# A 512-step recurrent cell: five bf16-part steps of eight instead of four, and other shares of the input's products

## The chip, the core and the metric

The kernel runs on one core of a Trainium2 chip. The metric is the time of one execution on the device, in microseconds (us); the kernel before takes 1638.1 us, the median of 3 runs (1637.6 to 1639.26). Its profile is one such execution, of 1637.59 us.

The engines that matter are TensorE (PE: matmuls, and PEld, its weight loads), VectorE (DVE), ScalarE (ACT), GpSimd (POOL) and SyncE (SP, which issues most DMAs).

## The reference

Eight sequences of 512 steps go through a gated cell with 512 hidden units; the result is added to the input.

```python
def step(h, x_t):
    fused = sigmoid(concatenate([x_t, h], -1) @ w_W + w_b)
    hidden_state, output_state = split(fused, 2, axis=-1)     # r and z below
    memory_state = x_t @ wx_W + wx_b + hidden_state * (h @ wh_W + wh_b)
    h_new = output_state * h + (1.0 - output_state) * tanh(memory_state)
    return h_new, h_new
_, hs = scan(step, h0, swapaxes(x, 0, 1))
out = x + swapaxes(hs, 0, 1)
```

What needs x alone can be computed ahead. What needs h (three products of 512 x 512 in each step: for r, for z and for the memory) cannot start before the step before has ended.

## The kernel before

**Steps, groups, octets.** The main loop runs over the 512 steps i. Four steps make a group and share banks of the accumulator memory (PSUM): their eight batch rows each lie below one another in 32 rows. Two groups make an octet. Below, o is the octet's number (0 to 63) and u the step's place in it (0 to 7); the group of u = 0 to 3 is called even, that of u = 4 to 7 odd.

**The products with h.** The 512 units are in four chunks k (the contraction) and four column groups j (the output, 32 rows of PSUM each, one beside the other on the PE array). For each k and j the weights have 384 columns, in three banks: A (192: z, r and memory of half A of the units), B (128: r and memory of half B) and C (64: z of half B). `ORDER` fixes the order in each step: A0 B0 A1 A2 A3 B1 B2 B3 C0 C1 C2 C3, where the digit is k. A0 and B0 need the new state's first chunk, A1 its second, and so on. The trace counts two MATMULs and two weight loads for each fp32 product.

**C in parts.** `in_parts(i)` tells in which steps C is made otherwise: the state and the weights are each split into three bf16 parts. The state's parts (`split`) are the left operand: 3 parts of 8 batch rows, 24 columns, loaded once per k and j. The weights' three parts (`high(wb)`, `w2`, `w3`) are each run against it: the first by `mm`, the other two by `kept` (line 219 of the kernel before), which does not load the left operand again. The result lies in 24 rows, and a TENSOR_REDUCE on DVE adds the three (`tzs<-tzB`). For that a step needs 64 columns of its own in bank `cs`, `cell(i)`; steps in fp32 of the odd group share 64 columns. Before, steps u = 0 to 3 are made in parts from step 24 on. `split` is made on POOL at the end of the step before, four TENSOR_TENSORs (two for each half of the units); `w2` and `w3` are made once on POOL, a pair in each of the steps 12 to 19.

**x in shares.** The products with x of a whole octet are made ahead, by a scheme with seven products where eight would be needed (`product`, `SLOTS`): seven slots of two products, of 384 columns each, 2688 columns in all. `SHARE` gives the columns that each step of the octet computes, behind C; `x_step` walks along them. A share that crosses the end of a slot becomes two pieces. The sums between the products lie on ACT and DVE (copies and additions of 64 x 384), and `spread`, `spread_c` and `turn_x` bring the finished rows to where the steps start: `spread_c` writes the rows of one step, chosen by a mask, into its cell for C.

**One step after the last product A.** DVE transposes A's three pieces (`tr<-A`, `md1A<-A`, `tz<-A`), ACT takes the sigmoids, DVE combines (`m`, two scans), ACT takes tanh, DVE makes the new state of half A (`hT<-hd0A`, chunks 0 and 1), and the same follows for half B out of banks B and C (`hT<-hd0B`, chunks 2 and 3). PE works on B, C and the x share meanwhile.

**What sets the order.** Nothing is reordered: `Flow` records the operations as the program is written, works out the semaphore waits from the memory that they touch, and issues them in that order on each engine. So almost every instruction carries line 255 (257 in the changed kernel), that of the issuing loop, and must be told apart by its tiles. An access to a PSUM bank also waits for the last access of another engine to the same rows of that bank.

Of the kernel before, what the change touches and what calls it, by code (L numbers as in the profile page):

```python
# [15 lines left out]
NQ = 4  # L16
GS = 4
HS = 12
B = 8
HU = 64  # L20
# [24 lines left out]
    [("P7", 0), ("P6", 1)],  # L45
]

SHARE = [384, 384, 384, 384, 288, 288, 288, 288]

XP = {"A": slice(0, 192), "X": slice(192, 320), "C": slice(320, 384), "B": slice(384, 512)}  # L50

# [213 lines left out]
def tile_cond_rnn_residual(  # L265
# [42 lines left out]
    T = NCH * TC  # L308
    NG = T // GS
    LAST = NG // 2 - 1  # L310
# [70 lines left out]
    NH = 2 * GS  # L381
# [40 lines left out]
    def state(hf, i, slot=2):  # L422
# [4 lines left out]
    cs = psum.tile([P, 512], F32, name="cs")  # L427
    wide = [{n: psum.tile([P, 512], F32, name=f"{n}{q}") for n in "AB"} for q in range(2)]
    banks = [
        {"A": wide[q]["A"][:, : BANKS["A"]],  # L430
         "B": wide[q]["B"][:, : BANKS["B"]],
         "C": cs[:, GS * HU : GS * HU + HU]}
        for q in range(2)
    ]
    xps = [psum.tile([P, 512], F32, name=f"xp{q}") for q in range(2)]
# [3 lines left out]
    def high(t_):  # L439
        return t_.bitcast(BF16)  # L440
# [41 lines left out]
    def keep(g):  # L482

        nc.vector.tensor_tensor(
            source(g)[:, XC], (piece if g == 2 else xps[g % 2])[:, XC], bias[:, XC], ALU.add
        )

    def source(g):

        return xps[g % 2] if g // 2 == LAST else (even, odd)[g % 2]  # L490

    def spread(g, names):

        for n in names:
            nc.scalar.copy(banks[g % 2][n], source(g)[:, XP[n]])

    def cell(i):
        return cs[:, HU * (i % GS) : HU * (i % GS) + HU] if i // GS % 2 == 0 else banks[1]["C"]

    def in_parts(i):  # L500
        return 3 * NH <= i < T and i // GS % 2 == 0

    def spread_c(g, steps_):

        for s in steps_:
            nc.scalar.activation(
                cell(GS * g + s), source(g)[:, XP["C"]], AF.Copy, scale=mask[:, s, :1]
            )

    def turn_x(g, hf):  # L510

        c0 = XP["X"].start + HU * hf
        nc.vector.transpose(
            md1[hf][g % 2][:, :, :, 1].rearrange("p n c -> p c n"), source(g)[:, c0 : c0 + HU]
        )

    def reg(r, c=XC):
        return xps[r[0]][r[1], c]
# [18 lines left out]
    def x_sum(o, n):  # L537

        t_ = [q[o % 2] for q in sx]
        a, b, op = [  # L540
            (x_half(o, 1, 0), x_half(o, 1, 1), ALU.add),
            (t_[0], x_half(o, 0, 0), ALU.subtract),
            (x_half(o, 0, 0), x_half(o, 1, 0), ALU.subtract),
            (x_half(o, 0, 1), t_[1], ALU.subtract),
        ][n]
        nc.gpsimd.tensor_tensor(t_[n], a, b, op)

    def product(o, name, k, c0, c1):

        if not 2 <= o < LAST:  # L550
            return
        t_ = [q[o % 2] for q in sx]
        to, lhs, rhs = {
            "P1": (AL, lambda: x_half(o, 0, 0), wx_of(0, 0)),
            "P2": (DE, lambda: t_[0], tw[0]),
            "P3": (BE, lambda: t_[1], tw[1]),
            "P4": (AL, lambda: x_half(o, 0, 1), wx_of(1, 0)),
            "P5": (GA, lambda: t_[2], tw[2]),
            "P6": (BE, lambda: t_[3], wx_of(1, 1)),
            "P7": (GA, lambda: x_half(o, 1, 1), tw[3]),  # L560
            "E": (None, lambda: t_[2], tw[2]),
        }[name]
        for j in range(2):
            r = slice(32 * j, 32 * j + 32)
            out_ = eps[r, c0:c1] if to is None else reg(to, slice(XC.start + c0, XC.start + c1))[r]
            mm(out_, lhs()[:, k], rhs[:, k, j, c0:c1], start=to is None and c0 == 0)
# [17 lines left out]

    def x_step(o, u):

        at = sum((SHARE * 2)[5 : u if u > 4 else u + 8]) - SHARE[5] // 3
        o += 2 if u > 4 else 1
        end = at + SHARE[u]
        while at < end:  # L590
            n, c0 = divmod(at, W)
            c1 = min(W, c0 + end - at)
            for pair_, (name, k) in enumerate(SLOTS[n % 7]):
                product(o + n // 7 - (n % 7 == 0 and pair_ == 0), name, k, c0, c1)
            at += c1 - c0
# [27 lines left out]
    for i in range(T):  # L623
# [8 lines left out]
        for n in (ORDER if i else FIRST).split():  # L632
            if n == "x":
                take(first[3], 1)
                continue
            bank, k = n[0], int(n[1])
            lhsT = hs[i % NH][:, k, :32, 2]
            for j in range(NQ):
                if bank == "C" and in_parts(i):
                    parts(cell(i)[32 * j : 32 * j + 24], i, k, j)  # L640
                else:
                    to = cell(i) if bank == "C" else ps[bank]
                    mm(to[32 * j : 32 * j + 32, :], lhsT, wh(bank, k, j))
        if T - 17 <= i < T - 5:
            take(last[i >= T - 11], 1)
        elif i > 4:
            x_step(*divmod(i, 2 * GS))
# [42 lines left out]
        def turn_z(hf):  # L690
            if hf and in_parts(i):
                tz = work.tile([P, 2, B], F32, tag="tzs", name=f"tzs_{i}")
                nc.vector.tensor_reduce(
                    tz, tzb[0].rearrange("p c (u b) -> p c b u", u=4), mybir.AxisListType.X, ALU.add
                )
            else:
                tz, _ = turned("z", hf)
            if hf == 0:
                inst = nc.vector.memset(idle[:, IDLE - 1 :], 0.0).ins
                nc.after(inst, h_done[0])  # L700
            act(hd0[hf][i % 2][:, :, :, 2].rearrange("p n c -> p c n"),
                tz,
                AF.Sigmoid,
                scale=-1.0,
            )
# [24 lines left out]
        o, u = divmod(i, 2 * GS)  # L730
# [24 lines left out]
        update(1, 1)  # L755
        if 0 < o < LAST and u == 1:
            spread(2 * o + 1, "C")
        if nxt and u in (6, 7):
            spread_c(2 * o + 2, (2 * u - 12, 2 * u - 11))
        for hf in range(2 if i < T - 1 else 0):  # L760
            act(state(hf, i + 1, 0), state(hf, i + 1), AF.Copy)
            if in_parts(i + 1):
# [6 lines left out]
                    ALU.subtract,  # L769
                )  # L770
                nc.gpsimd.tensor_tensor(t_[:, :, 2], t_[:, :, 0], high(t_)[:, :, 0, 1::2], ALU.subtract)
        if NH + GS <= i < NH + GS + 2 * NQ:
            k, n = (i - NH - GS) // 2, slice(i % 2 * 2, i % 2 * 2 + 2)
            for to, t_ in ((w2, wb[:, :, :, :HU]), (w3, w2)):
                nc.gpsimd.tensor_tensor(
                    to[:, k, n], t_[:, k, n], high(t_)[:, k, n, 1::2], ALU.subtract
                )
# [8 lines left out]
        if o == LAST:  # L786
            if u == 2:
                spread(2 * o + 1, "AB")
                turn_x(2 * o + 1, 0)
                turn_x(2 * o + 1, 1)  # L790
            elif u == 3:
                spread(2 * o + 1, "C")
        elif u == 0:
            if o == 0:
                spread(1, "A")
            if sums:
                nc.scalar.copy(reg(BE), reg(AL))
                nc.scalar.copy(both[LO], reg(DE))
                x_sum(o + 1, 3)
            turn_x(2 * o + 1, 0)  # L800
            turn_x(2 * o + 1, 1)
        elif u == 1:
            if sums:
                nc.scalar.copy(more[HI], eps)
            spread(2 * o + 1, "BC" if o == 0 else "A")
        elif u == 2:
            if sums:
                nc.vector.tensor_tensor(reg(GA), reg(BE), more[HI], ALU.add)
                nc.scalar.copy(even[LO, XC], reg(AL))
            if o:  # L810
                spread(2 * o + 1, "B")
        elif u == 3:
            if sums:
                nc.vector.tensor_tensor(odd[HI, XC], reg(GA), both[LO], ALU.add)
                nc.scalar.copy(both[HI], reg(DE))
            if two:
                x_sum(o + 2, 2)
        elif u == 4:
            if o == 0:
                keep(3)  # L820
            if two:
                nc.scalar.copy(reg(AL), bias[LO, XC])
                x_sum(o + 2, 0)
        elif u == 5:
            if sums:
                nc.vector.tensor_tensor(even[HI, XC], reg(BE), both[HI], ALU.add)
            if two:
                nc.scalar.copy(reg(DE), step_bias[HI])
        elif u == 6 and nxt:
            spread(2 * o + 2, "AB")  # L830
            turn_x(2 * o + 2, 0)
        elif u == 7 and nxt:
            if o:
                nc.scalar.copy(odd[LO, XC], reg(GA))
            turn_x(2 * o + 2, 1)
            if two:
                x_sum(o + 2, 1)
# [107 lines left out]
```

## Time and profile before

| what | value |
|---|---|
| median of 3 runs | 1638.1 us |
| the profiled execution | 1637.59 us |
| its span, first to last instruction | 1635.5 us |
| TensorE busy | 1625.4 us (99%) |
| its weight loads | 1397.4 us (85%) |
| ACT / DVE / POOL busy | 1254.0 / 1235.8 / 531.8 us |
| granted TensorE clock | 1.000 |
| DMA, mean over the span | 19 GB/s |

Some 2.1 us of the profiled execution lie outside the span. A busy PE is not a PE at its peak: ends of matmuls are modelled. The step's length is best read from the starts of `tr<-A`, the first thing that DVE does when bank A is finished: there is one in each step, and the time from one to the next holds the rest of the step's own work (B, C, x) and the next step's A. "Length of step u" below means that.

### The profile page before, as it was taken

What the parts mean: (1) busy time and instruction counts of PE and PEld (TensorE: products, weight loads), DVE (VectorE), ACT (ScalarE), POOL (GpSimd) and SP (SyncE); (2) the same over time, 40 slices, a digit from 0 to 9 for tenths busy, and PEclk for the clock granted to TensorE, in tenths of its full rate; (3) what the DMA queues carried; (4) which work ended last, traced back from release to release, by engine and by line L of the source; (5) the groups of instructions that cost most, each with busy time, mean ns of one, the idle gap of its engine ahead of it and who ended that gap; (6) DMA issues with size and microseconds to landing.
All of it is one profiled execution on the core that took longest, in us unless ns stands there. A gap on an engine that the chain in (4) does not pass through costs nothing.

```text
span 1635.5 us, 127307 instructions
## 1 busy us (share of the span) xinstructions
PE 1625.4 (99%) x58202; PEld 1397.4 (85%) x50394; DVE 1235.8 (76%) x9433; ACT 1254.0 (77%) x6188; POOL 531.8 (33%) x2272
## 2 busy tenths in 40 slices
PE   8999999999999999999999999999999999999998
PEld 5988898988888888888888888888888888988887
DVE  7777777777777777777777777777777777777776
ACT  4777777778777777777777777777777777777775
POOL 1323323333233333332333333323333333333332
PEclk9999999999999999999999999999999999999999
DMA  4000000000000000000000000000000000000000
GB/s 185 12 14 18 15 15 14 18 15 14 15 18 15 15 14 18 15 15 15 17 15 15 15 18 14 15 15 18 14 15 15 17 15 15 15 18 10 10 10 11
DMA packets 37297, 31.25 MB, mean 19 GB/s; under 512 B 4084, under 2 KB 35060, under 8 KB 36600
## 3 DMA queue, kind: packets, MB, share of 16 engines
q1 hardware_dynamic: 36576, 22.89, 4.5%
q8 instruction: 425, 6.96, 1.7%
q14 instruction: 144, 1.18, 0.2%
q10 hardware_dynamic: 152, 0.22, 0.0%
HBM read 14.70 MB, written 8.39 MB: 14 GB/s over the span
## 4 chain that ended last, share of the span: by engine, by line
PE 98%; DVE 1%; DMA 0%; ACT 0%; issue 0%; DVEq 0%; ACTq 0%; SPq 0%
PE A L255 41%; PE B L255 27%; PE xp L255 17%; PE cs L255 9%; PE cs L219 4%; PE eps L255 1%; DMA head<-in_xh_dram 0%; DVE tr L255 0%; DVE m L255 0%; DVE tw L255 0%; DVE hT L255 0%; DVE md1A L255 0%; DVE tz L255 0%; DVE md1B L255 0%; DVE even L255 0%
## 5 line engine op out<-in xcount | busy, mean ns | idle before, releaser
L255 PE MATMUL A<-wa,hT 128*32 128x192 f32 x16384 | 872.3, 327 | 3.2 <-DVE hT L255 3.1
L255 PEld LDWEIGHTS A<-wa,hT 128*32 128x32 f32 x16384 | 549.4, 122 | 189.8 <-DVE hT L255 132.1
L255 PE MATMUL B<-wb,hT 128*32 128x128 f32 x16384 | 652.0, 273 | 0.0
L255 PEld LDWEIGHTS B<-wb,hT 128*32 128x32 f32 x16384 | 542.5, 122 | 19.9 <-DMA wb<-in_wb_dram 0.3
L255 POOL TENSOR_TENSOR ot<-xin,hT 128x16 f32<-128x16 f32 x991 | 224.1, 250 | 598.8 <-DVE hT L255 596.8
L255 ACT ACTIVATE hT<-m 128x8 f32<-128x8 f32 x2048 | 349.2, 208 | 65.0 <-DVE m L255 64.1
L255 DVE STREAM_TRANSPOSE tr<-A 128x64 f32<-128x64 f32 x512 | 127.9, 250 | 291.9 <-PE A L255 285.8
L255 PE MATMUL xp<-tw,sx 128*32 128x384 f32 (+2 forms) x1464 | 264.0, 433 | 0.0
L255 POOL TENSOR_TENSOR split<-hT 128x32 f32<-128x32 f32 x488 | 126.0, 258 | 410.0 <-DVE m L255 397.9
L255 ACT ACTIVATE hT<-hT 128x16 f32<-128x16 f32 x1022 | 210.3, 225 | 50.1 <-DVE hT L255 47.8
L255 ACT ACTIVATE md0A<-tr 128x16 f32<-128x16 f32 x512 | 112.2, 219 | 165.4 <-DVE tr L255 158.8
L255 DVE TENSOR_TENSOR_SCAN hT<-hd0B,hT 128x24 f32<-128x24 f32 x1024 | 179.5, 204 | 75.7 <-ACT hT L255 52.4
L255 PE MATMUL xp<-wx,xin 128*32 128x384 f32 (+4 forms) x1348 | 218.3, 413 | 0.0
L255 DVE TENSOR_TENSOR_SCAN hT<-hd0A,hT 128x24 f32<-128x24 f32 x1024 | 198.3, 194 | 0.0
L255 PE MATMUL cs<-wb,hT 128*32 128x64 f32 x8576 | 173.0, 219 | 0.0
L255 PEld LDWEIGHTS cs<-wb,hT 128*32 128x32 f32 x8576 | 161.4, 122 | 0.0
L255 DVE TENSOR_TENSOR_SCAN m<-md0A,md1A 128x16 f32<-128x16 f32 x1024 | 142.3, 181 | 6.9
L255 DVE TENSOR_TENSOR_SCAN m<-md0B,md1B 128x16 f32<-128x16 f32 x1024 | 145.0, 163 | 0.6 <-issue 0.4
L255 ACT ACTIVATE hd0A<-tz 128x16 f32<-128x16 f32 x512 | 116.0, 227 | 20.9
L219 PE MATMUL cs<-w,split 128*24 128x64 bf16 x7808 | 129.9, 192 | 0.0
L255 PE MATMUL cs<-wb,split 128*24 128x64 bf16 x3904 | 122.2, 192 | 0.0
L255 POOL TENSOR_TENSOR split<-split 128x16 f32<-128x16 f32 x488 | 105.2, 216 | 38.2
(101 smaller groups left out, 2216.0 us busy)
## 6 DMA issues: line engine op xcount, KB each, us to landing
out_dram<-ot SPq DMA_DIRECT2D x128, 64.0 KB, 1.6
xin<-in_x_dram SPq DMA_DIRECT2D x112, 64.0 KB, 2.4
wx<-in_wx_dram SPq DMA_DIRECT2D x4, 768.0 KB, 7.5
wa<-in_wa_dram SPq DMA_DIRECT2D x4, 384.0 KB, 10.1
wb<-in_wb_dram SPq DMA_DIRECT2D x1, 1152.0 KB, 13.4
xin<-in_x_dram SPq DMA_DIRECT2D x3, 256.0 KB, 3.1
wb<-in_wb_dram SPq DMA_DIRECT2D x1, 384.0 KB, 13.8
head<-in_xh_dram ACTq DMA_DIRECT2D x1, 208.0 KB, 5.6
```

What stands on the lines that cost most here:

```text
L219: return t.add_instruction(mybir.InstMatmult(name=self.nc.get_next_instruction_name(), ins=[t.lower_ap(rhs), t.lower_ap(lhsT)], outs=[t.lo ...
L255: inst = getattr(self, item.op, getattr(engine, item.op, None))(*item.args, **item.kw)
```

## The change

Three edits. First, C of the odd group's first step (u = 4) is also made in parts. It has a cell of its own for that in `cs`, the fp32 steps' shared columns move 64 to the right, and `spread_c` writes that step's x rows into its cell (a further ACTIVATE in each octet, behind the updates of u = 2; in octet 0 in u = 1 and in the last one in u = 3). Second, the shares of x: 384 columns in u = 4 as in u = 0 to 3, and 256 in u = 5, 6 and 7; the start of the walk moves by 96 columns, so that u = 0 to 4 now fill one slot each. Third, the weights' parts are made in steps 8 to 15, and parts are used from step 16 on.

```diff
-SHARE = [384, 384, 384, 384, 288, 288, 288, 288]
+SHARE = [384, 384, 384, 384, 384, 256, 256, 256]
+
+EARLY = 0
...
-         "C": cs[:, GS * HU : GS * HU + HU]}
+         "C": cs[:, (GS + 1) * HU : (GS + 2) * HU]}
...
     def cell(i):
-        return cs[:, HU * (i % GS) : HU * (i % GS) + HU] if i // GS % 2 == 0 else banks[1]["C"]
+        n = i % NH
+        return cs[:, HU * n : HU * n + HU] if n <= GS else banks[1]["C"]
 
     def in_parts(i):
-        return 3 * NH <= i < T and i // GS % 2 == 0
+        return 2 * NH <= i < T and i % NH <= GS
...
-        at = sum((SHARE * 2)[5 : u if u > 4 else u + 8]) - SHARE[5] // 3
+        at = sum((SHARE * 2)[5 : u if u > 4 else u + 8]) - EARLY
...
         if 0 < o < LAST and u == 1:
             spread(2 * o + 1, "C")
+        if 0 < o < LAST and u == 2:
+            spread_c(2 * o + 1, (0,))
...
-        if NH + GS <= i < NH + GS + 2 * NQ:
-            k, n = (i - NH - GS) // 2, slice(i % 2 * 2, i % 2 * 2 + 2)
+        if NH <= i < NH + 2 * NQ:
+            k, n = (i - NH) // 2, slice(i % 2 * 2, i % 2 * 2 + 2)
...
             elif u == 3:
                 spread(2 * o + 1, "C")
+                spread_c(2 * o + 1, (0,))
...
             spread(2 * o + 1, "BC" if o == 0 else "A")
+            if o == 0:
+                spread_c(1, (0,))
```

Two places show what moves. The first is PE's queue from u = 4 on in an octet in the middle. Before, with `hT_71` the state of u = 4 and `hT_72` that of u = 5, `cs` bank C, `xp` and `eps` the banks of the x products:

```order
L255 MATMUL cs<-wb,hT_71 32x64 x16
L255 MATMUL xp_121<-tw_101,xin_138 32x288 x2
L255 MATMUL xp_120<-wx,sx_109 32x288 x2
L255 MATMUL A_118<-wa,hT_72 32x192 x4
L255 MATMUL B_119<-wb,hT_72 32x128 x4
L255 MATMUL A_118<-wa,hT_72 32x192 x12
L255 MATMUL B_119<-wb,hT_72 32x128 x12
L255 MATMUL cs<-wb,hT_72 32x64 x16
L255 MATMUL xp_121<-tw_101,xin_138 32x96 x2
L255 MATMUL xp_120<-wx,sx_109 32x96 x2
L255 MATMUL xp_121<-tw_101,xin_138 32x192 x2
L255 MATMUL eps<-tw_100,sx_106 32x192 x2
```

In the changed kernel the same stretch, from the last three of the 48 matmuls of u = 4's C (`split_75` the state's parts, `w_77` and `w_78` the weights' second and third part):

```order
L257 MATMUL cs<-wb,split_75 24x64
L221 MATMUL cs<-w_77,split_75 24x64
L221 MATMUL cs<-w_78,split_75 24x64
L257 MATMUL xp_121<-tw_101,xin_138 32x384 x2
L257 MATMUL xp_120<-wx,sx_109 32x384 x2
L257 MATMUL A_118<-wa,hT_72 32x192 x4
L257 MATMUL B_119<-wb,hT_72 32x128 x4
L257 MATMUL A_118<-wa,hT_72 32x192 x12
L257 MATMUL B_119<-wb,hT_72 32x128 x12
L257 MATMUL cs<-wb,hT_72 32x64 x16
L257 MATMUL xp_121<-tw_101,xin_138 32x256 x2
L257 MATMUL eps<-tw_100,sx_106 32x256 x2
```

The 16 fp32 products of u = 4's C became 48 in bf16, its x share went from 288 to 384 columns, and that of u = 5 from 288 in two pieces to 256 in one.

The second place is ACT's queue at the end of u = 2, from the last tanh (`hT_69<-m`) on; `md0A<-tr` is the first sigmoid of u = 3. Before:

```order
L255 ACTIVATE hT_69<-m_2_140 128x8
L255 ACTIVATE hT_70<-hT_70 128x8x2 x2
L255 COPY even<-xp_120 64x384
L255 COPY B_119<-odd 128x128
L255 ACTIVATE md0A_80<-tr_3_148 128x2x8
```

In the changed kernel:

```order
L257 ACTIVATE hT_69<-m_2_140 128x8
L257 ACTIVATE cs<-odd,mask 128x64
L257 ACTIVATE hT_70<-hT_70 128x8x2 x2
L257 COPY even<-xp_120 64x384
L257 COPY B_119<-odd 128x128
L257 ACTIVATE md0A_80<-tr_3_148 128x2x8
```

One ACTIVATE, the x rows of u = 4's cell, stands ahead of the two copies of the state.

## The prediction

> **What bounds the kernel now.** I read the page first: is one engine full, and does the chain that ended last stay on it?
>
> ```profile
> span 1635.5 us, 127307 instructions
> PE 1625.4 (99%) x58202; PEld 1397.4 (85%) x50394; DVE 1235.8 (76%) x9433; ACT 1254.0 (77%) x6188; POOL 531.8 (33%) x2272
> PE 98%; DVE 1%; DMA 0%; ACT 0%; issue 0%; DVEq 0%; ACTq 0%; SPq 0%
> ```
>
> The chain lies on PE for 98%. That says that PE sets the length of most steps, but not that each would shrink with PE's work: below PE's queue runs a loop through DVE and ACT (A, transposes, sigmoids, state, next A), and a step can't be shorter than that. So I next looked for the length of each step u, by the starts of `tr<-A` in DVE's timeline. This is octet 20 (first start: u = 0):
>
> ```profile
> 525.60 0.25 DVE L255 STREAM_TRANSPOSE tr<-A 128x64 f32<-128x64 f32 x1 [0.80 <-PE A L255]
> 528.79 0.25 DVE L255 STREAM_TRANSPOSE tr<-A 128x64 f32<-128x64 f32 x1 [0.55 <-PE A L255]
> 531.97 0.25 DVE L255 STREAM_TRANSPOSE tr<-A 128x64 f32<-128x64 f32 x1 [0.81 <-PE A L255]
> 535.14 0.25 DVE L255 STREAM_TRANSPOSE tr<-A 128x64 f32<-128x64 f32 x1 [0.17 <-PE A L255]
> 538.33 0.25 DVE L255 STREAM_TRANSPOSE tr<-A 128x64 f32<-128x64 f32 x1
> 541.43 0.25 DVE L255 STREAM_TRANSPOSE tr<-A 128x64 f32<-128x64 f32 x1 [0.96 <-PE A L255]
> 544.54 0.25 DVE L255 STREAM_TRANSPOSE tr<-A 128x64 f32<-128x64 f32 x1 [0.28 <-PE A L255]
> 547.65 0.25 DVE L255 STREAM_TRANSPOSE tr<-A 128x64 f32<-128x64 f32 x1 [0.82 <-PE A L255]
> 550.76 0.25 DVE L255 STREAM_TRANSPOSE tr<-A 128x64 f32<-128x64 f32 x1 [0.81 <-PE A L255]
> ```
>
> The four steps in parts with 384 columns take 538.33 - 525.60 = 12.73, 3.18 each; the four in fp32 with 288 take 3.10, 3.11, 3.11, 3.11, 12.43 in all. What PE does in them shows the chain of waits, for u = 4 (fp32) and then for u = 1 (parts; its rows between are C's single matmuls):
>
> ```profile
> 538.92 0.45 PE cs L255 x29
> 539.37 0.49 PE xp L255 x8
> 539.85 0.33 PE A L255 x8
> ```
>
> ```profile
> 529.38 0.01 PE cs L255 x2
> ...
> 529.74 0.65 PE xp L255 x8
> ```
>
> C costs 0.45 in fp32 and 529.74 - 529.38 = 0.36 in parts; 288 columns of x cost 0.49, 384 cost 0.65.
>
> A price for a column comes from steps that differ in nothing else. In octets 1 and 2 all steps are fp32; here are a step of 384 columns (the first pair of starts) and one of 288 (the second):
>
> ```profile
> 71.03 0.25 DVE L255 STREAM_TRANSPOSE tr<-A 128x64 f32<-128x64 f32 x1 [0.83 <-PE A L255]
> 74.30 0.25 DVE L255 STREAM_TRANSPOSE tr<-A 128x64 f32<-128x64 f32 x1 [0.86 <-PE A L255]
> ```
>
> ```profile
> 58.60 0.25 DVE L255 STREAM_TRANSPOSE tr<-A 128x64 f32<-128x64 f32 x1 [0.42 <-PE A L255]
> 61.71 0.25 DVE L255 STREAM_TRANSPOSE tr<-A 128x64 f32<-128x64 f32 x1 [0.96 <-PE A L255]
> ```
>
> 3.27 - 3.11 = 0.16 for 96 columns: 1.67 ns each, while PE sets the length. And 3.27 in fp32 against 3.18 in parts at 384 columns: parts are worth 0.09 a step.
>
> **Where the floor is.** The last octets have what the change makes: their x shares are of 256 columns, and there are none at all in the last steps. First steps 499 to 502 (u = 3 to 6; the first in parts, the others fp32):
>
> ```profile
> 1592.47 0.25 DVE L255 STREAM_TRANSPOSE tr<-A 128x64 f32<-128x64 f32 x1 [0.80 <-PE A L255]
> 1595.62 0.25 DVE L255 STREAM_TRANSPOSE tr<-A 128x64 f32<-128x64 f32 x1 [0.80 <-PE A L255]
> 1598.70 0.25 DVE L255 STREAM_TRANSPOSE tr<-A 128x64 f32<-128x64 f32 x1 [0.94 <-PE A L255]
> 1601.78 0.25 DVE L255 STREAM_TRANSPOSE tr<-A 128x64 f32<-128x64 f32 x1 [0.94 <-PE A L255]
> 1604.90 0.24 DVE L255 STREAM_TRANSPOSE tr<-A 128x64 f32<-128x64 f32 x1
> ```
>
> Then steps 507 (parts) and 508 (fp32), without any x:
>
> ```profile
> 1617.64 0.24 DVE L255 STREAM_TRANSPOSE tr<-A 128x64 f32<-128x64 f32 x1
> 1620.79 0.25 DVE L255 STREAM_TRANSPOSE tr<-A 128x64 f32<-128x64 f32 x1 [0.79 <-PE A L255]
> 1623.87 0.25 DVE L255 STREAM_TRANSPOSE tr<-A 128x64 f32<-128x64 f32 x1 [0.94 <-PE A L255]
> ```
>
> An fp32 step takes 3.08 with 256 columns and 3.08 with none. At 1.67 ns a column, 256 should have given 3.11 - 0.05 = 3.06 (3.105 - 0.053 = 3.052 unrounded). So 3.08 is the floor of the fp32 step, and 3.15 that of the step in parts, whose reduction on DVE comes on top. What holds the short step back shows around the first A, in u = 4 of octet 20 (288 columns) and in step 500 (256):
>
> ```profile
> 539.34 0.20 DVE L255 TENSOR_TENSOR_SCAN hT<-hd0A,hT 128x24 f32<-128x24 f32 x1
> ...
> 539.60 0.21 PEld L255 LDWEIGHTS A<-wa,hT 128*32 128x32 f32 x8 [0.28 <-DVE hT L255]
> ...
> 539.66 0.52 PE L255 MATMUL A<-wa,hT 128*32 128x192 f32 x8
> ```
>
> ```profile
> 1596.89 0.19 PEld L255 LDWEIGHTS A<-wa,hT 128*32 128x32 f32 x8 [0.28 <-DVE hT L255]
> 1596.90 0.53 PE L255 MATMUL A<-wa,hT 128*32 128x192 f32 x8
> ```
>
> In both, A's weight load starts 1.27 after `tr<-A` (538.33 and 1595.62), 0.06 behind the end of the state's scan. With 288 columns the first matmul starts 0.06 after it, behind x. With 256 it starts 0.01 after: x is done, PE follows its weight loads, and the rest of the gain is lost.
>
> **The change part by part.** I add up lengths of steps, in octets 2 to 60 (59 of them).
>
> u = 4 becomes what u = 0 to 3 are, parts with 384 columns: 3.18 for 3.10, +0.08. By terms: C -0.09, 96 columns +0.16. PE is what sets it, 0.03 above the floor of 3.15. On POOL, step u = 3 issues four more TENSOR_TENSORs, as u = 7 and u = 0 to 2 do already, at up to 0.26 each (a row further down): 1.0 us from about 1.85 after `tr<-A` on (533.82 - 531.97 in u = 2), so they end at about 2.9 of the step's 3.18, before the next C starts; behind them wait only the additions of the output and one sum for x. DVE's transpose of z and the reduction take the place of the plain transpose, as in u = 0 to 3.
>
> u = 5, 6 and 7 go from 3.11 to the floor, 3.08: -0.03 each. That u = 6 now has two pieces of 128 columns costs nothing beside a wait (u = 5 loses its second piece). Together 3.18 + 3 x 3.08 = 12.42 against 12.43: -0.01 per octet, x 59 = -0.6 us. The rows carry 0.01, so this is nought give or take as much.
>
> The further ACTIVATE at u = 2 is ACT's, at a mean of 0.30 by the first row here:
>
> ```profile
> L255 ACT ACTIVATE cs<-even,mask 128x64 f32<-128x64 f32 x188 | 51.3, 304 | 1.2
> ```
>
> ```profile
> 534.35 0.23 ACT L255 ACTIVATE hT<-hT 128x16 f32<-128x16 f32 x1 [0.15 <-DVE hT L255]
> ...
> 535.43 0.22 ACT L255 ACTIVATE md0A<-tr 128x16 f32<-128x16 f32 x1 [0.19 <-DVE tr L255]
> ```
>
> Ahead of the second state copy ACT is idle for 0.15 and ahead of the next sigmoid for 0.19, 0.34 together: it fits. Behind it stand two copies and u = 3's first sigmoid, for which DVE waits. With no cover at all u = 3 would grow by 0.30, 18 us over the octets; I take nought because the idle time is there.
>
> The edges. Octet 2 gets parts in u = 0 to 3: 4 x (3.18 - 3.27) = -0.3. Octet 1, still fp32, gets u = 4 at 3.27 and three steps at the floor: +0.16 - 0.09 = +0.07. In octets 62 and 63 u = 4 goes from the fp32 floor to that of parts: 2 x 0.07 = +0.14. The weights' parts are the same 16 POOL operations, four steps earlier, where POOL has nothing that anyone waits for; the last pair stands behind the first splits in step 15 and may be late once by some 0.1. Sum: -0.6 - 0.3 + 0.07 + 0.14 = **-0.7 us**, from 1637.6 to 1636.9 for the profiled execution; the median of the runs stands 0.5 above that execution, so 1637.4.
>
> A rule against the change, weighed. The 48 matmuls of C in parts take 0.36 here, 7.5 ns each. The Trainium skill, page "TensorE: Matmul & The Clock Gate", section on 56 ns not being 53.3, says that starts never come closer than about 25 ns however few columns a matmul has. By that C in parts would take 1.2 us and u = 4 would grow by a further 0.8; the trace contradicts it where four column groups run side by side, and I go by the trace.
>
> **Rivals.**
>
> *The short steps shrink by all their work (faster).* If the floor of 3.08 belonged to the last octets alone, u = 5 to 7 would be 3.055 each: 3.18 + 9.165 = 12.35, -0.08 per octet, -4.9, with the edges 1633.0. For it: those octets have other x products. Against: the weight load of octet 20 stands at the same 1.27 as in step 500, so the loop is as long there.
>
> *The short steps don't shrink (slower).* u = 5 to 7 also carry the sums between the products and the spreading of the next octet's x on ACT and DVE. If these hold them at 3.11, each octet pays +0.08: 4.7 us, 1642.8. It decides from 3.10 up: (3.18 + 9.30 - 12.43) x 60 = +3. For it: step 502 (u = 6), with 256 columns, took 1604.90 - 1601.78 = 3.12. Against: there the next `tr<-A` shows no wait for PE, because DVE itself was late, with an x transpose from PSUM that only the last octets have; elsewhere it reads SBUF, and DVE waits for PE by 0.28 and 0.82 at the end of u = 5 and 6 in octet 20.
>
> *POOL holds up DVE's state scans at u = 3 (slower).* If a split on POOL and a scan excluded each other, the scan of half B would start up to 0.26 to 0.5 late, and A's last products with it. After some 0.25 of slack that is up to 0.2 x 61 = 14 us, about 1650. The pair of scans at u = 2 beside splits, the first split there, and the pair at u = 3 without:
>
> ```profile
> 533.82 0.26 POOL L255 TENSOR_TENSOR split<-hT 128x32 f32<-128x32 f32 x1 [1.63 <-DVE m L255]
> ...
> 533.92 0.40 DVE L255 TENSOR_TENSOR_SCAN hT<-hd0B,hT 128x24 f32<-128x24 f32 x2
> ```
>
> ```profile
> 537.11 0.39 DVE L255 TENSOR_TENSOR_SCAN hT<-hd0B,hT 128x24 f32<-128x24 f32 x2
> ```
>
> 0.40 and 0.39: no such block. The Trainium skill, page "SBUF — State Buffer", section "Who interferes with whom", says that a DVE instruction with two SBUF inputs and a GpSimd one that reads SBUF do exclude each other; by that this rival would hold, and these rows speak against it.
>
> **How the numbers follow.** Forecast, within its own range: 0.77. All shrink: 0.11. None shrinks: 0.08. POOL: 0.02. Something else, such as rare pauses that no wait explains: 0.02. The forecast's own range: u = 4 at 3.17 to 3.19 (the lengths of u = 0 to 3 in octet 20) and the short steps at 3.07 to 3.09 give -0.05 to +0.03 per octet, -3.0 to +1.8 us, with the edges 1635.0 to 1639.8. The range given reaches a little towards both rivals, 1634.2 to 1640.2. A difference under 0.2% (3.3 us) can't be told from none here: faster by more than that 0.13, within it 0.76, slower 0.11.
>
> **What would show it.** u = 4 at 3.18, u = 5 to 7 at 3.08, the first A there directly behind its weight load; `md0A<-tr` of u = 3 still 0.28 after `tr<-A`; octet 2 shorter by 0.3. I am wrong if u = 5 to 7 stand at 3.05 to 3.06 or at 3.11, if u = 4 stands above 3.20, or if u = 3 grows (ACT or POOL).

## The result, and the profile after

The changed kernel takes 1642.2 us (median of 18 runs), the one before 1638.56 us beside it (18 runs). The ratio is 1.0022, with a 95% interval of 1.0015 to 1.0029: slower by 0.2%, where 1637.4 and no difference were forecast.

The page of the changed kernel, with its span, its busy times and two groups that moved:

```profile
span 1640.4 us, 126855 instructions
...
PE 1630.4 (99%) x58770; PEld 1320.2 (80%) x48850; DVE 1263.6 (77%) x9499; ACT 1273.1 (78%) x6252; POOL 595.0 (36%) x2536
...
L257 PEld LDWEIGHTS A<-wa,hT 128*32 128x32 f32 x16384 | 505.3, 123 | 250.3 <-DVE hT L257 178.9
...
L257 DVE TENSOR_TENSOR_SCAN m<-md0A,md1A 128x16 f32<-128x16 f32 x1024 | 148.6, 187 | 7.3
```

A's weight loads waited 132.1 us for DVE's new state before and wait 178.9 now. DVE's first scan took 181 ns in the mean (142.3 us in all) and takes 187: 6.3 us more over 1024 of them. Where that lies is told by the step lengths. The starts of `tr<-A` in octet 20, from u = 3 on:

```profile
535.26 0.25 DVE L257 STREAM_TRANSPOSE tr<-A 128x64 f32<-128x64 f32 x1 [0.17 <-PE A L257]
538.45 0.25 DVE L257 STREAM_TRANSPOSE tr<-A 128x64 f32<-128x64 f32 x1
541.72 0.25 DVE L257 STREAM_TRANSPOSE tr<-A 128x64 f32<-128x64 f32 x1 [0.79 <-PE A L257]
544.80 0.25 DVE L257 STREAM_TRANSPOSE tr<-A 128x64 f32<-128x64 f32 x1 [0.25 <-PE A L257]
547.89 0.25 DVE L257 STREAM_TRANSPOSE tr<-A 128x64 f32<-128x64 f32 x1 [0.80 <-PE A L257]
550.97 0.25 DVE L257 STREAM_TRANSPOSE tr<-A 128x64 f32<-128x64 f32 x1 [0.79 <-PE A L257]
```

u = 3 is 3.19 and u = 5 to 7 are 3.08, 3.09 and 3.08, as forecast. u = 4 is 541.72 - 538.45 = 3.27 where 3.18 was forecast. It is so throughout: here are the medians of each u over octets 3 to 60, worked out from such rows of both profiles (us). The last column is the sum of the eight medians, so single long steps don't enter it; below, "the octet" is this sum.

| kernel | u = 0 | 1 | 2 | 3 | 4 | 5 | 6 | 7 | octet |
|---|---|---|---|---|---|---|---|---|---|
| before | 3.180 | 3.185 | 3.181 | 3.183 | 3.105 | 3.110 | 3.110 | 3.105 | 25.159 |
| changed | 3.178 | 3.186 | 3.178 | 3.183 | 3.262 | 3.079 | 3.092 | 3.078 | 25.236 |

0.077 x 58 octets is 4.4 us of the 4.9 between the two spans. Of the rest, single overlong steps give 0.7 more, the first and last octets some 0.3 more, and the first `tr<-A` comes 0.5 earlier.

What happens in u = 4 shows in the timelines of DVE and POOL. First the kernel before: the sum for x that is issued in u = 4, and the pair of first scans of u = 4 (`tr<-A` at 538.33):

```profile
537.99 0.32 POOL L255 TENSOR_TENSOR sx<-xin 128x64 f32<-128x64 f32 x1
```

```profile
538.87 0.28 DVE L255 TENSOR_TENSOR_SCAN m<-md0A,md1A 128x16 f32<-128x16 f32 x2
```

The changed kernel, POOL (the first and the last of u = 3's splits, then what stands behind them), DVE, and the first weight load of A (`tr<-A` at 538.45):

```profile
537.13 0.26 POOL L257 TENSOR_TENSOR split<-hT 128x32 f32<-128x32 f32 x1 [1.65 <-DVE m L257]
...
538.05 0.22 POOL L257 TENSOR_TENSOR split<-split 128x16 f32<-128x16 f32 x1
538.22 0.33 POOL L257 TENSOR_TENSOR sx<-xin 128x64 f32<-128x64 f32 x1
538.50 0.47 POOL L257 TENSOR_TENSOR ot<-xin,hT 128x16 f32<-128x16 f32 x2
538.91 0.34 POOL L257 TENSOR_TENSOR sx<-xin 128x64 f32<-128x64 f32 x1
```

```profile
538.99 0.39 DVE L257 TENSOR_TENSOR_SCAN m<-md0A,md1A 128x16 f32<-128x16 f32 x2
```

```profile
539.83 0.19 PEld L257 LDWEIGHTS A<-wa,hT 128*32 128x32 f32 x8 [0.48 <-DVE hT L257]
```

The sum waits for nothing but its turn. Before, it started 0.34 ahead of `tr<-A` and was done by 538.31. Now the splits of u = 3 stand in front of POOL's other work, the sum starts 0.46 behind `tr<-A`, and the scan pair that begins in its midst takes 0.39 in place of 0.28. Singly, the first scan of the pair took 0.192 before and 0.296 now (median of 56 octets each), and it lies beside this sum in all 56. These 0.10 stand in the loop that sets the step's floor: the first A's weight load starts 1.38 behind `tr<-A` (539.83 - 538.45) and not 1.27. The floor of a step in parts was 3.15; with 0.10 to 0.11 more it is the 3.26 that is seen.

### The profile page after: what moved, and what is told of

It reads as the page before. It is cut to its first block, busy times and chain, and to the rows that moved or that the text cites. A ratio compares the mean times of both kernels' runs of the same rounds, so it can differ in the third digit from the quotient of the medians.

```text
span 1640.4 us, 126855 instructions
## 1 busy us (share of the span) xinstructions
PE 1630.4 (99%) x58770; PEld 1320.2 (80%) x48850; DVE 1263.6 (77%) x9499; ACT 1273.1 (78%) x6252; POOL 595.0 (36%) x2536
## 4 chain that ended last, share of the span: by engine, by line
PE 98%; DVE 1%; ACT 0%; issue 0%; DVEq 0%; SPq 0%
PE A L257 41%; PE B L257 27%; PE xp L257 18%; PE cs L257 8%; PE cs L221 5%; PE eps L257 0%; DVE tr L257 0%; DVE m L257 0%; DVE tw L257 0%; DVE hT L257 0%; DVE md1A L257 0%; DVE tz L257 0%; DVE md1B L257 0%; DVE even L257 0%; ACT cs L257 0%
## 5 line engine op out<-in xcount | busy, mean ns | idle before, releaser
L257 PEld LDWEIGHTS A<-wa,hT 128*32 128x32 f32 x16384 | 505.3, 123 | 250.3 <-DVE hT L257 178.9
L257 PE MATMUL B<-wb,hT 128*32 128x128 f32 x16384 | 639.6, 273 | 0.2
L257 PEld LDWEIGHTS B<-wb,hT 128*32 128x32 f32 x16384 | 520.9, 122 | 37.3 <-DMA wb<-in_wb_dram 1.1
L257 POOL TENSOR_TENSOR split<-hT 128x32 f32<-128x32 f32 x620 | 160.7, 259 | 516.2 <-DVE m L257 503.6
L257 PE MATMUL xp<-wx,xin 128*32 128x384 f32 (+2 forms) x1348 | 217.3, 413 | 0.0
L221 PE MATMUL cs<-w,split 128*24 128x64 bf16 x9920 | 161.3, 192 | 0.3 <-issue 0.3
L257 POOL TENSOR_TENSOR split<-split 128x16 f32<-128x16 f32 x620 | 134.7, 217 | 48.6
L257 PE MATMUL cs<-wb,split 128*24 128x64 bf16 x4960 | 151.7, 192 | 0.0
L257 PEld LDWEIGHTS cs<-wb,split 128*24 128x24 bf16 x4960 | 128.7, 92 | 16.5
L257 PE MATMUL cs<-wb,hT 128*32 128x64 f32 x6464 | 127.7, 219 | 0.0
```

Of the source, the lines that this page charges most:

```text
L221: return t.add_instruction(mybir.InstMatmult(name=self.nc.get_next_instruction_name(), ins=[t.lower_ap(rhs), t.lower_ap(lhsT)], outs=[t.lo ...
L257: inst = getattr(self, item.op, getattr(engine, item.op, None))(*item.args, **item.kw)
```

## The experiments

### The sum moved out of the way

In the changed kernel, `x_sum(o + 2, 0)` is issued behind the additions of the output of u = 4 and no longer ahead of them. Nothing else differs.

```diff
             if two:
                 nc.scalar.copy(reg(AL), bias[LO, XC])
-                x_sum(o + 2, 0)
...
         for hf in (1, 0):
             pool_done[i + 1] = add(hf, nc.gpsimd)
+        if u == 4 and two:
+            x_sum(o + 2, 0)
```

> The changed kernel with one operation on POOL moved: the sum for x that is issued in u = 4 (x_sum(o + 2, 0), written sx<-xin) stands behind the additions of the output of u = 4 and no longer ahead of them, so it runs some 2.5 us later. Theory (the four splits of u = 3 push this sum onto DVE's first scan of u = 4, and both read the state buffer): the scan of u = 4 is back at 0.19 from 0.30, u = 4 goes from 3.26 to 3.18, the time falls by about 5 us, to 1637 to 1638. Rival (u = 4 in parts with 384 columns costs 3.26 for a reason of its own, in PE or in the reduction on DVE): u = 4 stays at 3.26 and the time at 1642.

Measured: ratio to before 0.9999 (0.9991 to 1.0008). This chip ran the kernel before in 1644.35 us and this one in 1643.49, so only the ratio is to be read, not the forecast time. DVE's first scans and the length of u = 4:

```profile
540.06 0.25 DVE L257 STREAM_TRANSPOSE tr<-A 128x64 f32<-128x64 f32 x1
...
540.60 0.28 DVE L257 TENSOR_TENSOR_SCAN m<-md0A,md1A 128x16 f32<-128x16 f32 x2
...
543.24 0.25 DVE L257 STREAM_TRANSPOSE tr<-A 128x64 f32<-128x64 f32 x1 [0.82 <-PE A L257]
```

The pair is back at 0.28 and u = 4 at 3.18. The octet is 25.157, 0.078 below the changed kernel and 0.002 below the one before. The rival falls: C in parts with 384 columns at u = 4 costs what it costs elsewhere.

Once more, on another chip, beside the kernel before:

> The changed kernel with the sum moved, once more, beside the kernel before on the same chip. Theory: medians of the steps as in its first run (u = 4 at 3.18, octet at 25.16 as before), the ratio to before between 0.998 and 1.002, and what is left of the difference in pauses. Rival: a ratio of 0.997 or lower, from the octet's median or from octet 2.

The ratio was 0.999 (0.9981 to 0.9999), the octet 25.157 again. The two intervals overlap, and the profiled run had fewer overlong steps than others (below); a gain of more than 0.1% is excluded by the first, one of some 0.05% by neither.

### Something that does not read, in the sum's old place

With the sum moved, POOL got a memset of a scratch tile where the sum had stood.

```diff
+SCRATCH = 256
...
+    scratch = const.tile([P, SCRATCH], F32, name="scratch")
...
             if two:
                 nc.scalar.copy(reg(AL), bias[LO, XC])
+                nc.gpsimd.memset(scratch, 0.0)
```

> As the kernel with the sum moved, but in the sum's old place on POOL a memset of 128x256 into a scratch tile, about as long as the sum (estimate 0.32 from POOL's memsets of 128x768, 0.74, and 128x16, 0.13) and reading nothing. It lies on the same scan. Theory that it is POOL's reading that holds the scan up: scan 0.19, u = 4 at 3.18. Rival, that any busy POOL holds DVE's scan up: scan about 0.30, u = 4 at 3.26, time at 1642.

Measured: ratio 0.9989 (0.9979 to 0.9998), octet 25.153, u = 4 at 3.179. POOL and DVE in u = 4 (`tr<-A` at 537.58):

```profile
538.01 0.31 POOL L258 MEMSET scratch<- 128x256 f32 x1
```

```profile
538.11 0.28 DVE L258 TENSOR_TENSOR_SCAN m<-md0A,md1A 128x16 f32<-128x16 f32 x2
```

The memset runs from 0.10 before the first scan's start to 0.21 behind it, so it covers the scan whole, and the scan is not touched. Where a sum had 0.22 left when the scan started (in one octet of the changed kernel's second profile), the scan took 0.27. So it isn't a busy POOL that holds the scan up. What the memset lacks is inputs, which leaves a POOL operation that reads (the memset is another kind of operation too, and no other one that reads was put in this place). That is what the Trainium skill says, page "SBUF — State Buffer", section "Who interferes with whom": a DVE instruction with two SBUF inputs contends with a GpSimd one that reads SBUF, not with one that only writes. These runs agree.

### The cause alone, in the kernel before

The kernel before got four more POOL operations at the end of u = 3, of the splits' form, into a tile that nobody reads.

```diff
+        if 3 * NH <= i < T - 1 and i % NH == 3:
+            for hf in range(2):
+                ...                      # the two subtractions of a split, into spare
```

> The kernel before, with the suspected cause alone: four more operations on POOL at the end of each u = 3 from step 24 on, of the form of the splits, into a scratch tile that nobody reads. C of u = 4 stays fp32, the shares stay 384 and 288. Theory: the sum of u = 4 lands on the first scan of u = 4, the scan goes from 0.19 to 0.30, and u = 4 from 3.10 to about 3.18 (the fp32 floor of 3.08 and 0.11, less the 0.03 that PE's work covers): 0.08 x 60, so 4.5 to 5 us more than before. Rival (the cost comes with C in parts at u = 4): u = 4 stays at 3.10 and the time within 1 us of before.

Measured: ratio 1.0024 (1.0013 to 1.0034). u = 4, still fp32 with 288 columns:

```profile
540.28 0.33 POOL L255 TENSOR_TENSOR sx<-xin 128x64 f32<-128x64 f32 x1
```

```profile
539.81 0.25 DVE L255 STREAM_TRANSPOSE tr<-A 128x64 f32<-128x64 f32 x1
...
540.35 0.39 DVE L255 TENSOR_TENSOR_SCAN m<-md0A,md1A 128x16 f32<-128x16 f32 x2
...
543.01 0.25 DVE L255 STREAM_TRANSPOSE tr<-A 128x64 f32<-128x64 f32 x1 [0.93 <-PE A L255]
```

The sum lands on the scan, the pair takes 0.39, u = 4 goes to 3.20 here and to 3.18 in the median, 0.077 more than before: as much as the whole loss of the change, without the change.

### Each half of the change alone, and the changed kernel again

On the chip of that second run (kernel before: 1644.71 us) ran the changed kernel itself, the shares alone, and the parts alone.

> The changed kernel itself, beside the others of this call. Theory: u = 4 at 3.26 with the first scan of u = 4 at 0.30, so about 0.2 to 0.3% slower than before, 5 us above the kernel with the sum moved. Rival (the difference to before seen first was mostly chance of chip and run): within 0.1% of before.

Its ratio there was 1.0012 (0.9999 to 1.0024): lower than 1.0022, with an interval that reaches it but doesn't exclude the rival. The octet was 25.232, u = 4 at 3.255, the scan at 0.292. So the loss in the steps is nearly the same on this chip; the time of the whole tells less there, for the reason of the section after next.

The shares alone, in the kernel before:

```diff
-SHARE = [384, 384, 384, 384, 288, 288, 288, 288]
+SHARE = [384, 384, 384, 384, 384, 256, 256, 256]
...
-        at = sum((SHARE * 2)[5 : u if u > 4 else u + 8]) - SHARE[5] // 3
+        at = sum((SHARE * 2)[5 : u if u > 4 else u + 8]) - 0
```

> The kernel before with the shares of the change alone (384 in u = 4, 256 in u = 5 to 7, walk from a slot's start); C of u = 4 stays fp32, parts from step 24. Theory (PE sets u = 4, the loop through DVE sets the short steps): u = 4 at 3.265, u = 5 to 7 at 3.08, 3.09 and 3.08, the scan of u = 4 at 0.19; per octet +0.16 - 0.08 = +0.08, so 5 us above before. Rival (short steps shrink by their work): 3.055 each, octet unchanged, within 1 us of before.

```profile
539.15 0.25 DVE L255 STREAM_TRANSPOSE tr<-A 128x64 f32<-128x64 f32 x1
542.42 0.25 DVE L255 STREAM_TRANSPOSE tr<-A 128x64 f32<-128x64 f32 x1 [1.12 <-PE A L255]
545.50 0.25 DVE L255 STREAM_TRANSPOSE tr<-A 128x64 f32<-128x64 f32 x1 [0.25 <-PE A L255]
```

u = 4 takes 3.27 and u = 5 takes 3.08. Medians: 3.265, 3.081, 3.092, 3.078, octet 25.239, 0.080 above before, so 4.6 us in 58 octets as the theory has it. The ratio, 1.0005 (0.9993 to 1.0016), is lower than that and would by itself speak for the rival; u = 5 at 3.08 and not at 3.055 speaks against it. This profile has 4.5 us of overlong steps (below), that of the kernel before on this chip 8.4.

The parts alone, with the sum moved:

```diff
-SHARE = [384, 384, 384, 384, 384, 256, 256, 256]
+SHARE = [384, 384, 384, 384, 288, 288, 288, 288]
...
-EARLY = 0
+EARLY = 96
```

> C of u = 4 in parts and the weights' parts early, with the sum moved, and the shares of before (288 in u = 4 to 7). Theory: u = 4 goes from 3.105 to the floor of a step in parts, 3.15, although PE has less to do; u = 5 to 7 stay at 3.105 to 3.11; +0.045 x 60, less 0.3 in octet 2: 2 to 2.5 us above before. Rival (PE sets every step): u = 4 at 3.02, 5 us below before.

```profile
541.25 0.25 DVE L257 STREAM_TRANSPOSE tr<-A 128x64 f32<-128x64 f32 x1
544.40 0.25 DVE L257 STREAM_TRANSPOSE tr<-A 128x64 f32<-128x64 f32 x1 [0.80 <-PE A L257]
```

u = 4 takes 3.15 (median 3.155), more than in fp32 (3.105), although PE has 0.09 less to do: the floor of a step in parts. The octet is 25.205, 0.046 above before, 2.7 us in 58 octets. The ratio, 1.0028 (1.0015 to 1.0041), is more, 4.6 us, where 2 to 2.5 were forecast; what the rest is isn't known, and the profile is of the fastest of the ten runs. The rival, PE alone sets it, falls.

### Shares by the floors

If the floors are 3.15 and 3.08, the columns that PE does while it waits anyway could be moved. Two versions of the kernel with the sum moved tried that.

```diff
-SHARE = [384, 384, 384, 384, 384, 256, 256, 256]
+SHARE = [360, 384, 384, 384, 360, 272, 272, 272]
...
-EARLY = 0
+EARLY = 24
```

> The kernel with the sum moved, and shares by the floors: 360 columns in u = 0 and u = 4, 272 in u = 5 to 7, 384 still in u = 1 to 3 (the sums between the products fix these), and the walk starts 24 columns early. Theory: u = 0 and u = 4 go to their floor, 3.15, u = 5 to 7 stay at 3.08, 3.09 and 3.08: 25.10 per octet against 25.16 before, so 3.5 to 4 us faster than before, about 1634.5. Rival (the length of the steps in parts is set by something else than their columns): u = 0 and u = 4 stay at 3.18, the time within 1 us of before.

```profile
543.52 0.25 DVE L257 STREAM_TRANSPOSE tr<-A 128x64 f32<-128x64 f32 x1
546.68 0.25 DVE L257 STREAM_TRANSPOSE tr<-A 128x64 f32<-128x64 f32 x1 [0.79 <-PE A L257]
549.78 0.25 DVE L257 STREAM_TRANSPOSE tr<-A 128x64 f32<-128x64 f32 x1 [0.27 <-PE A L257]
552.87 0.25 DVE L257 STREAM_TRANSPOSE tr<-A 128x64 f32<-128x64 f32 x1 [0.80 <-PE A L257]
555.99 0.25 DVE L257 STREAM_TRANSPOSE tr<-A 128x64 f32<-128x64 f32 x1 [0.81 <-PE A L257]
```

Wrong by far: ratio 1.0082 (1.0067 to 1.0098). u = 4 is near its floor (3.16), but u = 5 and u = 7, which have a piece of 24 columns each, take 3.10 and 3.12 and not 3.08; u = 0 came down by 0.01 only, and why is open. The octet is 25.194, 0.037 above the kernel with 384 and 256 columns, 2 us in all. Overlong steps (below) give 9.6 us more than in that kernel's first profile; the last 1.6 us between the two spans lie ahead of octet 3.

The second avoids pieces under 48 columns:

```diff
-SHARE = [384, 384, 384, 384, 384, 256, 256, 256]
+SHARE = [384, 384, 384, 384, 336, 264, 280, 272]
...
-EARLY = 0
+EARLY = 48
```

> The kernel with the sum moved, with 336 columns in u = 4 and 264, 280 and 272 in u = 5, 6 and 7 (the walk starts 48 columns early; u = 0 to 3 stay at 384, so that only u = 5 gets a piece under 100 columns). Theory: u = 4 goes from 3.18 to the floor of 3.15, u = 5 to 7 stay within 0.01 of 3.08, 3.09 and 3.08; 25.13 per octet against 25.16 before, with the edges 2 us below before, 0.1%. Rival (small pieces cost more than their columns, as those of 24 columns did): u = 5 at 3.10 and no gain, within 1 us of before.

```profile
539.93 0.25 DVE L257 STREAM_TRANSPOSE tr<-A 128x64 f32<-128x64 f32 x1
543.08 0.25 DVE L257 STREAM_TRANSPOSE tr<-A 128x64 f32<-128x64 f32 x1 [0.79 <-PE A L257]
546.16 0.25 DVE L257 STREAM_TRANSPOSE tr<-A 128x64 f32<-128x64 f32 x1 [0.26 <-PE A L257]
```

Here the steps do what the theory has: u = 4 at 3.15, u = 5 at 3.08, the octet at 25.143, 0.017 below before. Yet the ratio is 1.0019 (1.0008 to 1.003). The smallest sum of medians of all kernels is not the fastest kernel, because of the overlong steps: with them, the median of whole octets is 25.29 there and 25.16 in the kernel before. No version beat both kernels clearly.

### Overlong steps

The kernel before was profiled once more, on the chip of the section before last.

> The kernel before, once more with a profile, on the chip of this call, to see how much of its time lies in pauses that no wait explains (2 us in its first profile) when a chip runs the same program some us slower. Steps of octets 3 to 60 should have the medians of the first profile within 0.005; a longer time should lie in single steps that are 0.1 to 0.6 too long. Rival: all steps are longer by the same small share.

It took 1644.02 us there. Its medians are those of the first profile within 0.003 (octet 25.162 against 25.159): the steps aren't longer, single ones are. I count the steps of octets 3 to 60 that are more than 0.06 above the median of their u, and what they exceed it by.

| kernel | overlong steps | us |
|---|---|---|
| before, first profile | 11 | 2.0 |
| changed, first profile | 14 | 2.6 |
| before, again | 32 | 8.4 |
| changed, again | 27 | 5.8 |
| sum moved; again | 43; 20 | 10.4; 4.5 |
| memset | 24 | 5.6 |
| pushed in the kernel before | 26 | 6.2 |
| shares alone; parts alone | 18; 36 | 4.5; 7.8 |
| shares with 24; with 48 | 68; 60 | 20.0; 15.2 |

In the groups of waits they stand under "issue", time in which an engine waits for nothing that the profile shows. The kernel before again, and then the shares with pieces of 24 columns (us in total, times, longest):

```profile
PEld xp L255 <- issue: 6.3, 24, 0.8
PEld cs L255 <- issue: 3.2, 9, 0.6
```

```profile
PEld xp L257 <- issue: 11.1, 35, 0.8
PEld cs L257 <- issue: 6.3, 17, 0.8
```

What they are isn't settled; a lead stands at the end.

## Why the prediction was wrong

**The step that failed** is in the part on u = 4, where the four more splits on POOL at the end of u = 3 were costed at nothing: "behind them wait only the additions of the output and one sum for x". That nobody waits for this sum soon is true. But I asked only who waits for it, not what it would run beside once it starts 0.8 later against the step. It landed on DVE's first scan of u = 4, in the loop that sets the floor, and cost 0.10 there; u = 4 became 3.26 and not 3.18, in each of some 60 octets (0.02 of the 0.10 lay under PE's work). The cause alone in the kernel before gave the same 0.077 per octet, and moving the one sum took all of it away.

**The POOL rival** was the right mechanism at the wrong place, with 0.02. I looked for it where the new operations run, at the scans of u = 3, and there it costs next to nothing: the pair of state scans, now beside splits, takes 0.39 as without them. It struck one step later, through an old operation that was pushed. (Its sum, 0.2 x 61, is 12 and not 14.)

My rows on the splits did not show that a split can't hold a scan up. They showed that little of the split is left when the scan starts: 534.08 - 533.92 = 0.16 of 0.26. The kernel before also had the other case, which I did not look for: in step 313 the scan started 0.05 into the split.

```profile
1009.00 0.26 POOL L255 TENSOR_TENSOR split<-hT 128x32 f32<-128x32 f32 x1 [1.43 <-DVE m L255]
```

```profile
1009.06 0.45 DVE L255 TENSOR_TENSOR_SCAN hT<-hd0B,hT 128x24 f32<-128x24 f32 x2
```

The pair took 0.45 there and not 0.39, and its first scan 0.26 where 0.21 is usual. With the sums it can be read more closely. In both profiles of the changed kernel and in the one with the cause alone, 176 first scans begin with more than 0.15 of a sum left, and each ends 0.04 to 0.05 behind that sum; four begin with less than 0.14 left and take 0.19, as alone. So what costs is not that the two overlap, but how much of POOL's operation is still to come.

**The floors** held. The short steps stand at 3.079, 3.092 and 3.078, forecast 3.08; neither the rival of 3.055 nor that of 3.11 came. (That the time, 1642.2, is near the 1642.8 of the second of them is chance.) In u = 5 the first A starts directly behind its weight load, as forecast (`tr<-A` at 541.72):

```profile
542.99 0.19 PEld L257 LDWEIGHTS A<-wa,hT 128*32 128x32 f32 x8 [0.29 <-DVE hT L257]
```

```profile
543.00 0.38 PE L257 MATMUL A<-wa,hT 128*32 128x192 f32 x4
```

The load starts 1.27 behind `tr<-A`. u = 6 is 0.013 above the others: its first scan starts 0.55 behind `tr<-A`, that of u = 5 and 7 at 0.535 to 0.538, in both kernels. Before, PE's work hid that; I overlooked it, and what causes it is open.

**The price of u = 4 in parts**, 3.18 with 384 columns, held once the sum was away, and so did the sum of the octet: 25.157 measured, -0.002 against before, where -0.01 was forecast.

**ACT's further ACTIVATE** cost nothing: u = 2 and u = 3 kept their length (3.178 and 3.183).

**The edges.** Octet 1's u = 4 came at 3.265 and u = 4 of octets 62 and 63 at 3.16, as forecast. In octet 2 only three of the four steps in parts got shorter. The first took 3.30:

```profile
70.68 0.25 DVE L257 STREAM_TRANSPOSE tr<-A 128x64 f32<-128x64 f32 x1 [0.77 <-PE A L257]
73.98 0.25 DVE L257 STREAM_TRANSPOSE tr<-A 128x64 f32<-128x64 f32 x1 [0.53 <-PE A L257]
```

I had allowed for some 0.1 there, should the last weights' parts be late, but left it out of the sum. Together the four came 0.20 shorter, where 0.3 was put down (4 x 0.09 is 0.36). POOL's row shows the same mechanism as in u = 4, a sum for x behind them, beside a scan pair of 0.42:

```profile
71.17 0.33 POOL L257 TENSOR_TENSOR sx<-sx,xin 128x64 f32<-128x64 f32 x1
```

```profile
71.21 0.42 DVE L257 TENSOR_TENSOR_SCAN m<-md0A,md1A 128x16 f32<-128x16 f32 x2
```

**The range**, 1634.2 to 1640.2, left out the result because its upper end stopped short of both slower rivals, and POOL's collision had two chances in a hundred.

## What to carry to other kernels

When operations are added to an engine with idle time, follow what is queued behind them to its new place and see what runs there on the other engines, and which of the two starts first; "nobody waits for it" is only half of the question. A step that two limits share, an engine's work and a loop of latencies, should be costed by both, and a run in which one limit is far off (here the last steps, without x) gives the other. Medians of single steps can tell a change of 0.01 us a step, where a whole time that differs by several us between chips cannot; but they leave out the single long steps, and a gain in medians alone (336 columns in u = 4) was no gain.

## What the runs showed of the hardware that was not expected

- A scan on DVE whose inputs both lie in the state buffer took 0.296 us and not 0.192 beside a POOL TENSOR_TENSOR of 128x64 with two inputs there; beside a memset of about the same length it took 0.192. The loss goes by what is left of POOL's operation when the scan starts: 0.10 with 0.25 left, 0.14 with 0.29 left (octet 2), nothing with less than 0.14 left. A split of 128x32 mostly has 0.16 left and costs 0.01; in step 41 of the changed kernel it had 0.24 left, and the scan took 0.295 and not 0.208. POOL's spans are rough, so these are distances within the profile.
- A piece of 24 columns beside one of 248 made a step 0.02 to 0.04 longer (3.102 and 3.115) than one piece of 272 (3.079); with 48 columns beside 216 the step stayed at its floor (3.082).
- The same program had 2.0 us of overlong steps in one profile and 8.4 in another, with equal medians. Most stand near transfers of one queue of the page, here that of the shares with pieces of 24 columns (packets, MB, share of 16 engines):

```profile
q8 instruction: 429, 7.03, 1.8%
```

  These are transfers of 16 KB, one every 3.85 us (median). Of the 67 overlong steps of that profile whose first late instruction could be found, 50 first fall behind 1.0 to 1.6 us after the end of such a transfer; by chance it would be some 10, the share of 0.6 in 3.85. In the kernel before, profiled again, it is 23 of 32. That would fit the loading of instructions, but nothing was tried on it, nor is it known why the kernels with small pieces have twice as many such steps.
